# Layer 2 ffn of a four-layer graph network: layernorm folded into the product, sum with the tanh on GpSimd

## Chip, cores and metric

One core of a Trainium2 chip runs the whole network. The metric is device time in microseconds of one execution. The engines are TensorE (PE; its weight loads are listed as PEld), VectorE (DVE), ScalarE (ACT), GpSimd (POOL) and SyncE (SP, which starts most transfers).

## What is computed

Four layers, each a graph part and a feed-forward part, act on X, 2,708 tokens of 256 features in f32; every part is fed with the layernorm of X and its result is added to X. The change touches only layer 2's feed-forward part, which applies one step thirty times to each token by itself:

```python
def step(h, _):
    h = h + 0.01 * jnp.tanh(h)
    h = h * jax.nn.sigmoid(h)
    h = _layernorm(h, ln_w, ln_b)
    h = jnp.einsum('bsc,dc->bsd', h, W) + b
    return (h, None)
x, _ = jax.lax.scan(step, x, None, length=N_ITERS)   # N_ITERS = 30
```

`_layernorm` subtracts the row's mean, multiplies by 1 / sqrt(variance + 1e-5), then by ln_w, and adds ln_b.

## The kernel before

X lies in SBUF as 22 tiles of 128 tokens by 256 features (tokens on partitions, `NT = 22`). The parts run one after the other in the code (`PHASES`), but the instructions of neighbouring parts overlap. The kernel is written in a tile framework: it records operations in program order with their dependencies, and a scheduler then fixes the order of each engine's queue before the run. This order need not be that of the code. On the chip every engine takes its own queue strictly in that order, and a waiting instruction holds up those behind it.

`l2_ffn` keeps the state in `Hs`, 22 tiles, and treats them as 11 pairs (`G = 11`); thirty steps make `ITERS * G = 330` pairs. First ln_w is multiplied into the weight (`Ww`), and ln_b times the weight is added to the bias. `layernorm` then fills Hs. Each pair runs through `s_tanh` and six stages, which hand their result on in `st`:

- `s_tanh` (L558): tanh of the pair on ACT, 128x512, into a buffer `th`.
- `s_silu` (L562, L563): DVE computes 0.01 th + hs in one instruction, ACT takes silu of it in place.
- `s_stats` (L570 to L572, and L114 through the helper `pow`): for each tile DVE's statistics and their aggregate give mean and variance (`sc_mv`); POOL adds epsilon and raises to the power -0.5 (`sc_r`).
- `s_norm` (L579, L581, L582): DVE computes -mean * r (`sc_m`); ACT normalizes the first tile of the pair, POOL the second, into `n`.
- `s_turn` (L590, L593): four transposes on PE into PSUM (`psT`), one copy on ACT to SBUF (`nT`).
- `s_mix` (L600): four products of 128x128 by 128x256 on PE, listed as eight MATMUL, into one PSUM tile (`psN`).
- `s_bias` (L117 through the helper `tt`): DVE adds the bias on reading PSUM and writes hs.

The loop goes over ticks. In tick T the stages are called for pairs T-6, T-4, T-5, T-3, T-2, T-1 in this order, then s_tanh for pair T:

```python
for tick in range(total + len(stages)):
    for k in (6, 4, 5, 3, 2, 1):
        if 0 <= tick - k < total:
            st[tick - k] = stages[k - 1](tick - k, st[tick - k])
    if tick < total:
        st[tick] = s_tanh(tick)
```

After the loop, 11 additions on DVE (L117) put Hs onto X. All `th`, `n` and `nT` come from one pool of 11 buffers (`two`); psT and psN have four PSUM buffers each; the small `sc_` tiles have four. A pair of tiles reads what was written for it 11 ticks earlier.

Of the kernel before, what the change touches and what calls it, by code (L numbers as in the profile page):

```python
# [37 lines left out]
class Net:  # L38
    """Tokens lie on partitions: token n is row n % 128 of tile n // 128. X is the residual stream."""
# [40 lines left out]
    def bcast(self, name, n, tag=None, pool=None, row=0):  # L80
        """A row of an input on every partition."""
        src = self.a[name]
        pool = pool or self.const
        t = pool.tile([P, n], F32, name="bc_" + name, tag=tag or "bc_" + name)
        self.nc.sync.dma_start(
            t, bass.AP(tensor=src.tensor, offset=src.offset + row * n, ap=[[0, P], [1, n]])
        )
        return t

    def cols(self, name, k):  # L90
        """An input that the host laid out as [128, k]."""
        t = self.const.tile([P, k], F32, name="co_" + name, tag="co_" + name)
        self.nc.sync.dma_start(t, self.a[name])
        return t

    def mat(self, src, k, n, tag, pool=None):
        """A [k * 128, n] matrix with its rows on partitions."""
        t = (pool or self.wp).tile([P, k, n], F32, name=tag, tag=tag, bufs=3 if tag in ("w1", "w2") else 2)
        self.nc.sync.dma_start(t, src.rearrange("(k p) n -> p k n", p=P))
        return t  # L100

    def pair(self, name, shape=(2, D), parts=P):
        """Room for two tiles of tokens."""
        t = self.two.tile([P, 2 * D], F32, name=name, tag="two")
        t = t[:parts, : int(np.prod(shape))]
        return t if len(shape) == 1 else t.rearrange("p (a b) -> p a b", b=shape[1])

# [17 lines left out]
    def moments(self, mv, g0, g1):  # L125
        """Mean and variance of each token of tiles g0..g1 of X."""
        nc = self.nc
        for t in range(g0, g1):
            p = rows(t)
            st = self.tmp.tile([P, 6], F32, name="bst", tag="bst", bufs=4)  # L130
            nc.vector.bn_stats(st[:p], self.X[:p, t, :])
            nc.vector.bn_aggr(mv[:p, t, :], st[:p])

    def layernorm(self, scale_of, sink=None, into=None):
        """For each pair of tiles: sink(t0, scaled (x - mean), as [128, 2, 256]); kept in `into`."""
# [18 lines left out]
    def rstd(self, out, var, g0, g1):  # L154
        """1 / sqrt(var + eps)."""
        ve = self.tmp.tile([P, g1 - g0], F32, name="ve", tag="ve")
        self.ts(ve, var, EPS, ALU.add)
        self.pow(out, ve, self.mhalf)

    def transpose_into(self, ZT, gamma=None, beta=None):  # L160
        """A sink that puts the features of a pair of tiles on partitions."""
# [22 lines left out]
    def token_matmul(self, ZT, W, t, n, m=P):  # L184
        """Tile t's rows times W [128, 2, n], on token partitions."""
        ps = self.psB.tile([P, n], F32, name="psM", tag="psB")
        for c in range(KD):
            self.nc.tensor.matmul(ps[:m], lhsT=ZT[:, c, t * P : t * P + m], rhs=W[:, c, :],  # L188
                                  start=(c == 0), stop=(c == KD - 1))
        return ps  # L190

# [1 line left out]
    def chunk_dma(self, b, j0, move):  # L193
        """Calls move(m, c) for each part of a chunk: m cuts it from an [N, N] matrix, c from a tile."""
# [9 lines left out]
    def adj_chunks(self, b, src):  # L204
        """Chunks of src [N, N] for output tokens of block b: (first row tile, tile, parts)."""
# [8 lines left out]
    def aggregate(self, weights, R, w, done, src=None):  # L214
        """sum_j weights[j, i] R[j]; weights(b, j0, adj tile, parts, n) gives the chunk's weights."""
# [25 lines left out]
    def ramp(self, E):  # L241
        """E, E - 1, ... 1 on every partition: the earlier expert is the larger."""
        r = self.const.tile([P, E], F32, name=f"rev{E}", tag=f"rev{E}")
        self.nc.gpsimd.iota(r, pattern=[[-1, E]], base=E, channel_multiplier=0,
                            allow_small_or_imprecise_dtypes=True)
        return r
# [7 lines left out]
    def first_max(self, l, E, rev, m, oh, at=None):  # L254
        """The largest of E and a one-hot of its first place."""
# [9 lines left out]
    def top2(self, l, E):  # L265
        """Weights of all experts: softmax over the two largest, 0 elsewhere."""
# [31 lines left out]
    def logits(self, lhs, rhs, bias, E):  # L298
        """lhs: per tile, the chunks of stationary operands; rhs: the chunks of moving ones."""
# [11 lines left out]
    def add_weighted_bias(self, wf, name, E):  # L311
        """X += sum_e w_e b_e."""
# [19 lines left out]
    def hidden(self, W, src, kc, nh, n, func, bias, tag, k0=0):  # L332
        """func(W.T src + bias), features on partitions: nh blocks of 128 by n tokens."""
# [11 lines left out]
    def add_expert(self, h, nh, W, b0, k, wf, e):  # L345
        """X += w_e (h.T W) for the k tiles from b0."""
# [11 lines left out]
    def l0_gnn(self):  # L358
# [29 lines left out]
        def reciprocals(b, j0, at, parts, n):  # L388
            """1 / r of layer 1's weights, with r >= 1 as 0 and 1e-18 added to every r: it changes
            only those whose weight, exp(-2 (1/r - 1)^2), is 0 anyway."""  # L390
# [141 lines left out]
    def l2_ffn(self):  # L532
        nc, a = self.nc, self.a
        ITERS = 30
        lw, lb = self.cols("L2_ffn_ln_w", KD), self.cols("L2_ffn_ln_b", KD)
        bias = self.bcast("L2_ffn_b", D, tag="rowbc")
        WT = self.mat(a["L2_ffn_WT"], KD, D, "w3")
        # (n w + lb) W.T + b = n (w W.T) + (lb W.T + b), n the normalized row.
# [6 lines left out]
        Ww = self.const.tile([P, KD, D], F32, name="Ww", tag="Ww")  # L545
        for c in range(KD):
            self.ts(Ww[:, c, :], WT[:, c, :], lw[:, c : c + 1], ALU.mult)

        Hs = self.big.tile([P, NT, D], F32, name="Hs", tag="R")
        self.layernorm(self.rstd, into=Hs)  # L550
        G = NT // 2
        st = {}
        hs = lambda s: Hs[:, 2 * (s % G) : 2 * (s % G) + 2, :]
        tiny = lambda name, shape: self.tmp.tile([P, *shape], F32, name=name, tag=name, bufs=4)

        def s_tanh(s):
            th = self.pair("th")
            nc.scalar.activation(th, hs(s), AF.Tanh)  # L558
            return th

        def s_silu(s, th):
            nc.vector.scalar_tensor_tensor(th, th, 0.01, hs(s), op0=ALU.mult, op1=ALU.add)  # L562
            nc.scalar.activation(th, th, AF.Silu)  # L563
            return th

        def s_stats(s, g):
# [5 lines left out]
            nc.gpsimd.tensor_scalar(r, mv[:, :, 1], EPS, 1.0, op0=ALU.add, op1=ALU.mult)  # L572
            self.pow(r, r, self.mhalf)
            return g, mv, r

        def s_norm(s, gmr):
            g, mv, r = gmr
            m = tiny("sc_m", (2,))
            nc.vector.scalar_tensor_tensor(m, mv[:, :, 0], -1.0, r, op0=ALU.mult, op1=ALU.mult)  # L579
            n = self.pair("n")  # L580
            nc.scalar.activation(n[:, 0, :], g[:, 0, :], AF.Identity, bias=m[:, 0:1], scale=r[:, 0:1])  # L581
            nc.gpsimd.tensor_scalar(n[:, 1, :], g[:, 1, :], r[:, 1:2], m[:, 1:2], op0=ALU.mult,  # L582
                                    op1=ALU.add)
            return n

        def s_turn(s, n):
            ps = self.psB.tile([P, KD, 2 * P], F32, name="psT", tag="psB")
            for c in range(KD):
                for j in range(2):
                    nc.tensor.transpose(ps[:, c, j * P : (j + 1) * P], n[:, j, c * P : (c + 1) * P],  # L590
                                        self.ident)
            nT = self.pair("nT", (KD, 2 * P))
            nc.scalar.copy(nT, ps)  # L593
            return nT

        def s_mix(s, nT):
            ps = self.psA.tile([P, 2, D], F32, name="psN", tag="psA")
            for j in range(2):
                for c in range(KD):
                    nc.tensor.matmul(ps[:, j, :], lhsT=nT[:, c, j * P : (j + 1) * P],  # L600
                                     rhs=Ww[:, c, :], start=(c == 0), stop=(c == KD - 1))
            return ps

        def s_bias(s, ps):
            self.tt(hs(s), ps, bias.unsqueeze(1).to_broadcast([P, 2, D]), ALU.add)

        stages = [s_silu, s_stats, s_norm, s_turn, s_mix, s_bias]
        total = ITERS * G
        for tick in range(total + len(stages)):
            # A pair's transposes go before the products of the pair ahead, which cover their copy.  # L610
            for k in (6, 4, 5, 3, 2, 1):
# [4 lines left out]
        for t0 in range(0, NT, 2):  # L616
            self.tt(self.X[:, t0 : t0 + 2, :], Hs[:, t0 : t0 + 2, :], self.X[:, t0 : t0 + 2, :],
                    ALU.add)

# [1 line left out]
    def artanh(self, out, x):  # L621
        """0.5 (log1p(x) - log1p(-x)), log1p(u) = ln(w) u / (w - 1) with w = 1 + u (u where w is 1)."""
# [18 lines left out]
    def tanh_over(self, out, n, raw):  # L641
        """out = tanh(n) / n with n = max(raw, 1e-15)."""
# [6 lines left out]
    def ball(self, f, raw):  # L649
        """The factor that brings a row of norm raw into the ball: min(1, maxnorm / norm)."""  # L650
# [4 lines left out]
    def log_factor(self, out, f, raw):  # L655
        """artanh(n) / n, n = max(f * raw, 1e-15): the factor of logmap0 for a row of norm f * raw."""
# [14 lines left out]
    def l3_gnn(self):  # L671
# [6 lines left out]
        # The bias as a point of the ball.  # L678
# [12 lines left out]
        # mx = z W.T, its squared norm and its product with the bias.  # L691
# [12 lines left out]
        # |z| = sqrt(D var) / sqrt(var + eps)  # L704
# [17 lines left out]
        # Moebius sum of s mx and hb: ca mx + cb hb.  # L722
# [38 lines left out]
        # expmap0, proj, logmap0, relu, expmap0, proj: one factor of relu(u) for each token.  # L761
# [19 lines left out]
    def l3_ffn(self, out):  # L781
# [30 lines left out]
        # Each token's place among its expert's tokens, counted from 1.  # L812
# [20 lines left out]
        # A token past the capacity is written to a row of its own that no expert reads.  # L833
# [124 lines left out]
```

## Time and profile before

| quantity | us |
|---|---|
| three runs | 3749.0, 3742.19, 3748.62 |
| their median | 3748.62 |
| span of the profiled execution, first to last instruction | 3735.1 |
| difference of the median to the span | 13.5 |
| first tanh of the loop / last start of a product (L600) | 2075.1 / 2975.3 |

The profiled execution's time outside its span is not listed by the profile; the three runs lie 7.1 to 13.9 us above the span.

In the window 2100 to 2900 us, in the middle of the loop, the engines are busy, out of 800 us: PE 743.9, DVE 659.3, ACT 665.9, POOL 574.3, at a granted TensorE clock of 1.00. The mean durations there, in us, of one instruction:

| line, engine | what | number | one |
|---|---|---|---|
| L600 PE | product, 128x256 | 2640 | 0.380 |
| L590 PE | transpose, 128x128 | 1320 | 0.294 |
| L570 DVE | statistics, 128x256 | 660 | 0.405 |
| L571 DVE | aggregate | 660 | 0.169 |
| L562 DVE | 0.01 th + hs, 128x512 | 330 | 0.686 |
| L117 DVE | bias, 128x512 from PSUM | 330 | 0.671 |
| L579 DVE | sc_m, 128x2 | 330 | 0.161 |
| L558, L563 ACT | tanh, silu, 128x512 | 330 each | 0.615, 0.624 |
| L581 ACT | n, 128x256 | 330 | 0.600 |
| L593 ACT | copy, 128x512 from PSUM | 330 | 0.586 |
| L582 POOL | n, 128x256 | 330 | 0.801 |
| L572 POOL | epsilon, 128x2 | 330 | 0.413 |
| L114 POOL | power, 128x2 | 330 | 0.699 |

Durations of neighbours on one engine overlap somewhat: the next instruction starts before the last has left the engine. In the lists of waits a line reads: engine, tile and line that waited, the releaser, total us, times, longest us. In a timeline or a chain: start us, duration us, engine, tile, line. In the page's slices each digit is the busy share of one fortieth of the span, in tenths.

### The profile page before, as it was taken

The page shows a single profiled execution, that of the slowest core. Times are in us where ns is not written, and L with a number is a line of the kernel's source. Part 1 is how long each engine was busy: PE and PEld are TensorE (multiplying, and loading weights), DVE is VectorE, ACT ScalarE, POOL GpSimd, SP SyncE. Part 2 cuts the span into 40 slices and gives each one's busy share as a digit, 9 for nine tenths or more (in the row PEclk, how much of TensorE's full clock was granted, in tenths as well). Part 3 has the DMA queues.
Part 4 walks back from the last instruction along what each step waited for, and adds up shares of the span by engine and source line. Part 5 has one row for each costly group of instructions (what it writes and reads, how often), then busy time and mean ns, then how long its engine had stood idle before and what let it go on. Part 6 is the DMA issues. An engine that isn't in the chain of part 4 may idle for free.

```text
span 3735.1 us, 38081 instructions
## 1 busy us (share of the span) xinstructions
PE 3315.3 (89%) x13384; PEld 2346.6 (63%) x13384; DVE 1721.5 (46%) x4185; ACT 1445.2 (39%) x2458; POOL 931.8 (25%) x1224
## 2 busy tenths in 40 slices
PE   7988989999999999999999899999999859945782
PEld 5655556666667885555688566666666648733551
DVE  6999982111113112211401688888888850040005
ACT  2433451121222463222200588888888630011110
POOL 3323220000000000000200477777777510021004
PEclk9999987999999998999999999999999979957896
DMA  4333330000000352000154100000000015402222
GB/s 150 128 116 123 125 99 31 12 23 12 12 6 12 113 147 60 9 15 17 41 145 128 32 1 1 1 1 1 1 1 1 2 31 143 119 10 76 88 78 68
DMA packets 135083, 203.52 MB, mean 54 GB/s; under 512 B 10699, under 2 KB 59685, under 8 KB 134893
## 3 DMA queue, kind: packets, MB, share of 16 engines
q1 hardware_dynamic: 132812, 195.54, 17.4%
q0 software_dynamic: 2080, 5.55, 0.4%
q8 instruction: 106, 1.74, 0.2%
q14 instruction: 85, 0.69, 0.1%
HBM read 159.23 MB, written 41.83 MB: 54 GB/s over the span
## 4 chain that ended last, share of the span: by engine, by line
PE 55%; POOL 17%; DVE 14%; issue 9%; DMA 4%; ACT 1%; POOLq 0%; SPq 0%; DVEq 0%; ACTq 0%
PE acc L223 20%; PE psH L340 17%; PE psY L352 11%; POOL sc_r L114 6%; POOL n L582 5%; DVE sc_bs L570 4%; POOL sc_r L572 4%; DMA xb<-slots 3%; DVE inv L396 3%; PE psY L877 2%; DVE sc_m L579 1%; POOL e L413 1%; PE psS L406 1%; PE psY L325 1%; PE psM L188 1%
## 5 line engine op out<-in xcount | busy, mean ns | idle before, releaser
L223 PE MATMUL acc<-R,adj 128*128 128x256 f32 (+3 forms) x2904 | 654.3, 383 | 35.9 <-DVE R L121 35.9
L223 PEld LDWEIGHTS acc<-R,adj 128*128 128x128 f32 (+3 forms) x2904 | 527.0, 186 | 162.9 <-issue 51.3
L600 PE MATMUL psN<-Ww,nT 128*128 128x256 f32 x2640 | 625.9, 380 | 0.7 <-ACT nT L593 0.7
L600 PEld LDWEIGHTS psN<-Ww,nT 128*128 128x128 f32 x2640 | 476.8, 191 | 52.4 <-ACT nT L593 1.1
L354 DVE SCALAR_TENSOR_TENSOR X<-psY,wf,X 128x256 f32<-128x256 f32 x308 | 147.3, 483 | 756.2 <-PE psY L352 756.2
L342 ACT ACTIVATE hA<-psH,co_L_ffn_b 128x512 f32<-128x512 f32 (+2 forms) x256 | 164.3, 642 | 761.0 <-PE psH L340 761.0
L340 PE MATMUL psH<-ZT,w 128*128 128x512 f32 (+1 forms) x1056 | 435.9, 562 | 0.0
L114 POOL TENSOR_TENSOR lnscale<-ve,mhalf 128x4 f32<-128x4 f32 (+1 forms) x36 | 34.8, 965 | 1509.2 <-DVE ve L121 1502.3
L396 DVE RECIPROCAL inv<-inv 128x1024 f32<-128x1024 f32 (+3 forms) x72 | 377.8, 5285 | 5.7 <-ACT inv L395 5.4
L590 PE MATMUL psT<-ident,n 128*128 128x128 f32 x1320 | 254.1, 294 | 76.4 <-POOL n L582 39.0
L340 PEld LDWEIGHTS psH<-ZT,w 128*128 128x128 f32 x1056 | 201.9, 192 | 184.7 <-issue 176.3
L352 PE MATMUL psY<-w,hA 128*128 128x256 f32 x1408 | 311.7, 379 | 0.0
L352 PEld LDWEIGHTS psY<-w,hA 128*128 128x128 f32 x1408 | 267.5, 190 | 53.4 <-issue 19.1
L582 POOL TENSOR_SCALAR n<-th,sc_r,sc_m 128x256 f32<-128x256 f32 x330 | 264.3, 801 | 133.3 <-DVE sc_m L579 66.0
L590 PEld LDWEIGHTS psT<-ident,n 128*128 128x128 f32 x1320 | 143.9, 140 | 238.2 <-ACT n L581 165.5
L558 ACT ACTIVATE th<-Hs 128x512 f32<-128x512 f32 x330 | 202.9, 615 | 220.6 <-DVE Hs L123 220.6
L223 PE MATMUL acc<-R,e 128*128 128x257 f32 x968 | 238.3, 398 | 51.5 <-POOL e L413 29.9
L223 PEld LDWEIGHTS acc<-R,e 128*128 128x128 f32 x968 | 180.2, 192 | 119.5 <-POOL e L413 59.1
L570 DVE BATCH_NORM_STATS2 sc_bs<-th 128x6 f32<-128x256 f32 x660 | 252.9, 405 | 0.0
L562 DVE SCALAR_TENSOR_TENSOR th<-th,Hs 128x512 f32<-128x512 f32 x330 | 226.3, 686 | 24.7 <-ACT th L558 24.7
L114 POOL TENSOR_TENSOR sc_r<-sc_r,mhalf 128x2 f32<-128x2 f32 x330 | 230.7, 699 | 27.5
L581 ACT ACTIVATE n<-th,sc_m,sc_r 128x256 f32<-128x256 f32 x330 | 198.0, 600 | 85.4 <-DVE sc_m L579 75.0
(259 smaller groups left out, 3750.3 us busy)
## 6 DMA issues: line engine op xcount, KB each, us to landing
adj<-in_adjT SPq DMA_DIRECT2D x150, 512.0 KB
inv<-inv SPq DMA_DIRECT2D x50, 512.0 KB
adj<-inv SPq DMA_DIRECT2D x50, 512.0 KB
w<-in_L_ffn_w SPq DMA_DIRECT2D x32, 512.0 KB
w<-in_L_ffn_W SPq DMA_DIRECT2D x16, 512.0 KB
w<-in_L_ffn_expert_w SPq DMA_DIRECT2D x18, 256.0 KB
adj<-in_adjT SPq DMA_DIRECT2D x30, 148.0 KB
adj<-in_adjT SPq DMA_DIRECT2D x15, 256.0 KB
```

The lines of the kernel that those rows point to most:

```text
L114: self.nc.gpsimd.tensor_tensor(out, base, half[:, :k], op=ALU.pow)
L223: nc.tensor.matmul(acc[s][:ps, :w], lhsT=wt[:pj, k, s * P : s * P + ps], rhs=R[:pj, jt, :w], start=(jt == 0), stop=(jt == NT - 1))
L340: nc.tensor.matmul(ps, lhsT=W[:, c, f * P : (f + 1) * P], rhs=src(c), start=(c == 0), stop=(c == kc - 1))
L352: nc.tensor.matmul(py, lhsT=h[:, f, j * P : (j + 1) * P], rhs=W[:, f, :], start=(f == 0), stop=(f == nh - 1))
L396: nc.vector.reciprocal(o, o)
L558: nc.scalar.activation(th, hs(s), AF.Tanh)
L562: nc.vector.scalar_tensor_tensor(th, th, 0.01, hs(s), op0=ALU.mult, op1=ALU.add)
L570: nc.vector.bn_stats(bs, g[:, j, :])
L581: nc.scalar.activation(n[:, 0, :], g[:, 0, :], AF.Identity, bias=m[:, 0:1], scale=r[:, 0:1])
L582: nc.gpsimd.tensor_scalar(n[:, 1, :], g[:, 1, :], r[:, 1:2], m[:, 1:2], op0=ALU.mult, op1=ALU.add)
L590: nc.tensor.transpose(ps[:, c, j * P : (j + 1) * P], n[:, j, c * P : (c + 1) * P], self.ident)
L600: nc.tensor.matmul(ps[:, j, :], lhsT=nT[:, c, j * P : (j + 1) * P], rhs=Ww[:, c, :], start=(c == 0), stop=(c == KD - 1))
```

## The change

The mean is no longer subtracted from the rows: since the product is linear, the columns of the scaled weight are centred once ahead of the loop (`V`, by a product with a constant 1/256 and a subtraction), so that a row's mean drops out of the product. The factor r of each row is applied when PSUM is read, together with the bias: `s_out` is one DVE instruction per tile, psN * r + bias. `s_norm` is gone, and the transposes read the output of silu. The statistics go into `s_turn`; epsilon is added on ACT, the power stays on POOL.

The state Hs is kept 100 times as large (`UP`): then the sum is th + hs without a factor, and GpSimd computes it in a stage of its own (`s_sum`); tanh and silu scale their input by 1/100 in the same instruction, and V and the bias carry the factor 100. The scale of the first layernorm carries it too. The stages are now s_sum, s_silu, s_turn, s_mix, s_out, called for T-5, T-3, T-4, T-2, T-1. The addition to X is done by DVE in s_out of the last step, with 1/100.

```diff
         self.tt(bias, ps, bias, ALU.add)
-        Ww = self.const.tile([P, KD, D], F32, name="Ww", tag="Ww")
+        self.ts(bias, bias, UP, ALU.mult)
+        V = self.const.tile([P, KD, D], F32, name="V", tag="V")
         for c in range(KD):
-            self.ts(Ww[:, c, :], WT[:, c, :], lw[:, c : c + 1], ALU.mult)
+            self.ts(V[:, c, :], WT[:, c, :], lw[:, c : c + 1], ALU.mult)
+        mean = self.pair("mean", (P,))
+        self.ts(mean, self.ones, 1.0 / D, ALU.mult)
+        ps = self.psB.tile([P, D], F32, name="psM", tag="psB")
+        for c in range(KD):
+            nc.tensor.matmul(ps, lhsT=mean, rhs=V[:, c, :], start=(c == 0), stop=(c == KD - 1))
+        for c in range(KD):
+            self.tt(V[:, c, :], V[:, c, :], ps, ALU.subtract)
+            self.ts(V[:, c, :], V[:, c, :], UP, ALU.mult)
+
+        eps = self.const.tile([P, 1], F32, name="eps", tag="eps")
+        nc.gpsimd.memset(eps, EPS)
...
-        self.layernorm(self.rstd, into=Hs)
+        def scale(out, var, g0, g1):
+            self.rstd(out, var, g0, g1)
+            self.ts(out, out, UP, ALU.mult)
+
+        self.layernorm(scale, into=Hs)
...
-            nc.scalar.activation(th, hs(s), AF.Tanh)
+            nc.scalar.activation(th, hs(s), AF.Tanh, scale=1.0 / UP)
             return th
 
+        def s_sum(s, th):
+            nc.gpsimd.tensor_tensor(th, th, hs(s), op=ALU.add)
+            return th
+
         def s_silu(s, th):
-            nc.vector.scalar_tensor_tensor(th, th, 0.01, hs(s), op0=ALU.mult, op1=ALU.add)
-            nc.scalar.activation(th, th, AF.Silu)
+            nc.scalar.activation(th, th, AF.Silu, scale=1.0 / UP)
             return th
 
-        def s_stats(s, g):
+        def s_turn(s, g):
             mv, r = tiny("sc_mv", (2, 2)), tiny("sc_r", (2,))
...
-            nc.gpsimd.tensor_scalar(r, mv[:, :, 1], EPS, 1.0, op0=ALU.add, op1=ALU.mult)
+            nc.scalar.activation(r, mv[:, :, 1], AF.Identity, bias=eps)
             self.pow(r, r, self.mhalf)
-            return g, mv, r
-
-        def s_norm(s, gmr):
-            g, mv, r = gmr
-            m = tiny("sc_m", (2,))
-            nc.vector.scalar_tensor_tensor(m, mv[:, :, 0], -1.0, r, op0=ALU.mult, op1=ALU.mult)
-            n = self.pair("n")
-            nc.scalar.activation(n[:, 0, :], g[:, 0, :], AF.Identity, bias=m[:, 0:1], scale=r[:, 0:1])
-            nc.gpsimd.tensor_scalar(n[:, 1, :], g[:, 1, :], r[:, 1:2], m[:, 1:2], op0=ALU.mult,
-                                    op1=ALU.add)
-            return n
...
-                    nc.tensor.transpose(ps[:, c, j * P : (j + 1) * P], n[:, j, c * P : (c + 1) * P],
+                    nc.tensor.transpose(ps[:, c, j * P : (j + 1) * P], g[:, j, c * P : (c + 1) * P],
                                         self.ident)
...
-        def s_bias(s, ps):
-            self.tt(hs(s), ps, bias.unsqueeze(1).to_broadcast([P, 2, D]), ALU.add)
-
-        stages = [s_silu, s_stats, s_norm, s_turn, s_mix, s_bias]
+        def s_out(s, pr):
+            ps, r = pr
+            for j in range(2):
+                nc.vector.scalar_tensor_tensor(hs(s)[:, j, :], ps[:, j, :], r[:, j : j + 1], bias,
+                                               op0=ALU.mult, op1=ALU.add)
+            if s >= (ITERS - 1) * G2:
+                x = self.X[:, 2 * (s % G2) : 2 * (s % G2) + 2, :]
+                nc.vector.scalar_tensor_tensor(x, hs(s), 1.0 / UP, x, op0=ALU.mult, op1=ALU.add)
+
+        stages = [s_sum, s_silu, s_turn, s_mix, s_out]
...
-            for k in (6, 4, 5, 3, 2, 1):
+            for k in (5, 3, 4, 2, 1):
...
-        for t0 in range(0, NT, 2):
-            self.tt(self.X[:, t0 : t0 + 2, :], Hs[:, t0 : t0 + 2, :], self.X[:, t0 : t0 + 2, :],
-                    ALU.add)
```

`G2` is the former `G`, `gT` the former `nT`. What else the diff holds are comments.

More of the change, by code (lines that the diff above doesn't have):

```diff
@@ L534, in l2_ffn @@
         ITERS = 30
+        UP = 100.0
         lw, lb = self.cols("L2_ffn_ln_w", KD), self.cols("L2_ffn_ln_b", KD)
@@ L544, in l2_ffn @@
         self.tt(bias, ps, bias, ALU.add)
-        Ww = self.const.tile([P, KD, D], F32, name="Ww", tag="Ww")
+        self.ts(bias, bias, UP, ALU.mult)
+        V = self.const.tile([P, KD, D], F32, name="V", tag="V")
         for c in range(KD):
-            self.ts(Ww[:, c, :], WT[:, c, :], lw[:, c : c + 1], ALU.mult)
-        Hs = self.big.tile([P, NT, D], F32, name="Hs", tag="R")
-        self.layernorm(self.rstd, into=Hs)
-        G = NT // 2
+            self.ts(V[:, c, :], WT[:, c, :], lw[:, c : c + 1], ALU.mult)
[9 more added lines that the diff above has]
+        nc.gpsimd.memset(eps, EPS)
+        Hs = self.big.tile([P, NT, D], F32, name="Hs", tag="R")
+        def scale(out, var, g0, g1):
+            self.rstd(out, var, g0, g1)
+            self.ts(out, out, UP, ALU.mult)
+        self.layernorm(scale, into=Hs)
+        G2 = NT // 2
         st = {}
-        hs = lambda s: Hs[:, 2 * (s % G) : 2 * (s % G) + 2, :]
+        hs = lambda s: Hs[:, 2 * (s % G2) : 2 * (s % G2) + 2, :]
         tiny = lambda name, shape: self.tmp.tile([P, *shape], F32, name=name, tag=name, bufs=4)
@@ L571, in s_stats @@
                 nc.vector.bn_aggr(mv[:, j, :], bs)
-            nc.gpsimd.tensor_scalar(r, mv[:, :, 1], EPS, 1.0, op0=ALU.add, op1=ALU.mult)
+            nc.scalar.activation(r, mv[:, :, 1], AF.Identity, bias=eps)
             self.pow(r, r, self.mhalf)
-            return g, mv, r
-        def s_norm(s, gmr):
-            g, mv, r = gmr
-            m = tiny("sc_m", (2,))
-            nc.vector.scalar_tensor_tensor(m, mv[:, :, 0], -1.0, r, op0=ALU.mult, op1=ALU.mult)
-            n = self.pair("n")
-            nc.scalar.activation(n[:, 0, :], g[:, 0, :], AF.Identity, bias=m[:, 0:1], scale=r[:, 0:1])
-            nc.gpsimd.tensor_scalar(n[:, 1, :], g[:, 1, :], r[:, 1:2], m[:, 1:2], op0=ALU.mult,
-                                    op1=ALU.add)
-            return n
-        def s_turn(s, n):
             ps = self.psB.tile([P, KD, 2 * P], F32, name="psT", tag="psB")
@@ L589, in s_turn, with s_mix @@
                 for j in range(2):
-                    nc.tensor.transpose(ps[:, c, j * P : (j + 1) * P], n[:, j, c * P : (c + 1) * P],
+                    nc.tensor.transpose(ps[:, c, j * P : (j + 1) * P], g[:, j, c * P : (c + 1) * P],
                                         self.ident)
[L592 to L596, printed above, removed]
+            gT = self.pair("gT", (KD, 2 * P))
+            nc.scalar.copy(gT, ps)
+            return gT, r
+        def s_mix(s, gr):
+            gT, r = gr
             ps = self.psA.tile([P, 2, D], F32, name="psN", tag="psA")
@@ L599, in s_mix @@
                 for c in range(KD):
-                    nc.tensor.matmul(ps[:, j, :], lhsT=nT[:, c, j * P : (j + 1) * P],
-                                     rhs=Ww[:, c, :], start=(c == 0), stop=(c == KD - 1))
-            return ps
-        def s_bias(s, ps):
-            self.tt(hs(s), ps, bias.unsqueeze(1).to_broadcast([P, 2, D]), ALU.add)
-        stages = [s_silu, s_stats, s_norm, s_turn, s_mix, s_bias]
-        total = ITERS * G
+                    nc.tensor.matmul(ps[:, j, :], lhsT=gT[:, c, j * P : (j + 1) * P],
+                                     rhs=V[:, c, :], start=(c == 0), stop=(c == KD - 1))
+            return ps, r
+        def s_out(s, pr):
[7 more added lines that the diff above has]
+        stages = [s_sum, s_silu, s_turn, s_mix, s_out]
+        total = ITERS * G2
         for tick in range(total + len(stages)):
-            for k in (6, 4, 5, 3, 2, 1):
+            for k in (5, 3, 4, 2, 1):
                 if 0 <= tick - k < total:
```

## The prediction

> **What bounds the kernel now.** First the page's busy shares in 40 slices, to place the change in time.
>
> ```profile
> PE   7988989999999999999999899999999859945782
> ...
> DVE  6999982111113112211401688888888850040005
> ACT  2433451121222463222200588888888630011110
> POOL 3323220000000000000200477777777510021004
> PEclk9999987999999998999999999999999979957896
> ```
>
> Slices 24 to 31 are the only long stretch in which four engines are all busy: with parts of their neighbours this is the loop of layer 2's ffn (first tanh at 2075.1 us, last product at 2975.9), 330 pairs of tiles. PE shows 9, but that share is modelled, so I read who waits, in the window 2100:2900.
>
> ```profile
> PEld psT L590 <- ACT n L581: 137.2, 297, 1.0
> DVE sc_m L579 <- POOL sc_r L114: 117.4, 299, 0.5
> POOL sc_r L572 <- DVE sc_mv L571: 67.8, 150, 0.8
> ACT n L581 <- DVE sc_m L579: 66.9, 149, 0.5
> PEld psT L590 <- POOL n L582: 66.2, 158, 0.4
> ```
>
> PE waits for the normalized rows n, those for sc_m, and that for the power on POOL. Then the chain of waits for a few microseconds out of the middle:
>
> ```profile
> 2440.28 0.20 POOL sc_r L572
> ...
> 2440.56 0.72 POOL sc_r L114
> ...
> 2441.30 0.17 DVE sc_m L579
> ...
> 2441.66 1.06 POOL n L582
> ...
> 2442.80 0.65 POOL sc_r L572
> ...
> 2443.53 0.71 POOL sc_r L114
> ...
> 2444.26 0.16 DVE sc_m L579
> 2444.42 0.66 DVE sc_bs L570 x2
> ...
> 2445.64 0.20 POOL sc_r L572
> ```
>
> No PE is in it: statistics, epsilon, power, sc_m and n hand over between DVE and POOL, and the picture repeats after 2445.64 - 2440.28 = 5.36 us, two pairs: **2.68 us a pair**, and 330 x 2.683 = 885 us. How fast PE could go is seen at the loop's start, while pairs are still in store: its transposes begin at 2094.68, 2096.85 and 2099.01, so **2.16 us a pair**. The clock there is 1.00 in the window's row.
>
> **The change, part by part.** Durations are from the group rows unless said.
>
> *Removed, per pair.* On POOL L572 (0.41) and L582 (0.80); on DVE L562 (0.69), L579 (0.16) and the wide L117 (0.67); on ACT L581 (0.60). With them goes the loop shown above: the power's result is now read only by s_out, two stages later, and the transposes read g itself. What is late next is worked out below.
>
> *Added, per pair.* (1) POOL: th + hs, 128x512 with two SBUF inputs. The nearest rows are the same shape: L526 1.27 (median, DVE running beside it) and L413 1.27. I take 1.27. (2) ACT: epsilon onto 128x2. Not in the trace; ACT's 128x22 takes 0.22, its 128x256 0.42 to 0.60. I take 0.20; at 0.42 the round trip below grows by 0.22, 0.11 a pair. (3) DVE: two s_out from PSUM, 128x256; L383 has exactly this form, 0.48 each, and successive ones may start about 0.40 apart (the wide ones, 0.68 long, let the next start after 0.61). The scales 1/100 on Tanh and Silu ride in the same instruction: nothing.
>
> *Sums per pair after.* PE unchanged, 2.16. POOL 1.27 + 0.70 + two gaps of 0.08 (as between L582 and L572) = 2.13. ACT 0.62 + 0.62 + 0.59 + 0.20 = 2.03. DVE 2 x 0.31 + 2 x 0.09 + 2 x 0.48 = 1.76 (statistics by their starting distances). Nobody needs more than 2.16, against 2.68 now: the sums allow 0.52 x 330 = 172 us. PE and POOL are within 0.03 of each other, so waits decide what is left of it.
>
> *The added waits.* In POOL's queue the power of a pair stands ahead of a later pair's sum; it waits for r on ACT. Who waits behind it: the sum, then silu, then all. As the code orders it, power(s) goes in the tick in which sum(s+2) goes, so the round trip covers two pairs: sum 1.27, hand-over 0.05 (2120.44 to 2120.49, ACT to PE), silu 0.62, 0.05, two statistics and aggregates 0.87 (0.31 + 0.09 + 0.31 + 0.16 by the starts 2123.37, 2123.68 and 2123.76), 0.08, r 0.20, POOL's waking 0.20 (sc_m ended 2441.46, n began 2441.66), power 0.70, 0.09: **4.13 us, or 2.07 a pair** with nothing in the way. In its way on ACT can be a copy (0.48 from start to next start), as silu follows a copy in every second pair now: 4.61, **2.31 a pair**. I take that. The trace of before can't show the order in each queue after: it isn't the code's order even now (the wide L117, first in a tick by the code, runs behind the aggregates, at 2123.76 after 2123.68). So the bounds are 2.16 below and, above, the round trips in the rivals.
>
> *The port.* POOL's n takes 0.56 us at 2122.91 beside statistics, 1.06 at 2119.95 beside L562; its 128x2 L572 takes 0.19 and 0.64 likewise. So the removed L562, with two SBUF inputs, held POOL up by 0.45 to 0.50. The wide L117, with one input in PSUM, ran at 2121.60 beside a power of 0.70, the power's usual length. s_out is of that second kind, so I charge no contention. That POOL can hold DVE up too shows at 1821.60: four L123, SBUF to SBUF, take 2.33 us beside L526, 1.38 without it (2980.36). The Trainium skill, SBUF — State Buffer, section Who interferes with whom, has that rule: a VectorE instruction with two SBUF inputs locks a GpSimd one that reads SBUF out, one with at most one such input doesn't. It says nothing of the scalar column r, which s_out reads as well; if that counted, the last rival below would hold.
>
> *Against the change* stands first the row: the sum costs POOL 1.27 where DVE spent 0.69. The skill's GPSIMD Engine Reference, section Engine selection, tells one not to put two-input elementwise work on GpSimd at all; by its figure for 2,048 elements (section Elementwise — side-by-side cycle accounting: 4497 ns, a quarter is an estimated 1.12) POOL's sum of terms would be 1.98 instead of 2.13, and by its advice the move would be undone. Here POOL's total, not the single duration, is what counts.
>
> *Start and end.* Added ahead of the loop on DVE: bias 0.35, mean 0.80 (L542's shape), two subtractions 0.43, two scalings 0.35 = 2.7 us, and six of 0.16 on the scales, 3.7 in all; on PE four half-products, 0.9. DVE idles 23 us before 2073.45 and covers what doesn't need PE; uncovered it costs 3.7, and some four early sums beside the 18 instructions of L123 (5.90 us from 2075.38) could hold these up by 1 us each. Against that, the first L562 waits behind those 18 now, and the first transposes come at 2088.39, 13.3 us after the first tanh; the sum on POOL isn't behind them, and the power, sc_m and n (2086.48 to 2088.41) drop out ahead of PE: up to 9 us gained. I take 0 (bounds -9 and +8). At the end the 11 additions to X (0.68) lie between other DVE work now, and do so after: 0.
>
> **The sum.** 330 x (2.31 - 2.683) = -123 us. The profiled execution's span is 3735.1, so 3612 after; the three runs lie 7.1 to 13.9 us above that span, and their median of 3748.62 13.5. With the same 13.5 outside the span: **3626 us**, 3.3% less.
>
> **Rivals.**
>
> *A. PE sets the pace.* The order lets enough pairs stand in store, and each takes 2.16 as at 2094.68 to 2099.01: -173, **3576 us**. For it: the sums, and eleven buffers of pairs. Against: in the middle of the loop only 3 or 4 pairs lie between tanh and copy (by time 2601 195 tanh, 191 copies), and POOL's 2.13 leaves no slack.
>
> *B. The same round trip, with s_out in its way on DVE.* One of the two (0.40) ahead of the statistics: 5.01, 2.51 a pair, -57, **3692 us**. Both: 5.41, 2.70, which is about no change.
>
> *C. Slower: the round trip through PE takes the place.* If DVE takes s_out of an older pair ahead of each pair's statistics, as the code has it, and ACT takes r and copy ahead of silu, then: hand-over 0.05, transposes and products 2.38 (2123.46 to 2125.84), 0.05, two s_out 0.80, statistics 0.87, 0.08, r 0.20, copy 0.48, silu 0.62 = 5.53 for two pairs, **2.77 a pair**: +27, **3776 us**. It decides from 5.37 us for two pairs on. For it: both orders are the code's, and r is a new wait in ACT's queue with copy, silu and tanh behind it. Against: the queues are not in the code's order now.
>
> *D. Slower by the port.* If s_out counts as two SBUF readers, it and the sum exclude one another: POOL 2.13 + 0.80 = 2.93, +82, **3831 us**. Against: the undisturbed L117.
>
> *E. The change doesn't reach the end:* something else holds 2.68 (B with both). Within 0.2%, 7.5 us, which is about what a measurement can tell from no change here: 3748.
>
> **Chances.** Forecast (2.22 to 2.42 a pair) 0.40; A 0.17; B 0.14; E 0.04; C 0.16; D 0.09. Faster: 0.40 + 0.17 + 0.14 = 0.71; same 0.04; slower 0.25. The range takes in A below (3576) and C above (3776), with some of the start's bounds 3570 to 3785; D and what lies past either end, some 0.15 to 0.2, is left out.
>
> **What would show it.** Right: POOL's 128x512 sum at 1.27 and its power at 0.70, POOL the busiest or level with PE, the transposes waiting for silu, and that for POOL's sum; the start of successive transposes 2.3 apart. A: PE without idle before L590's successor, POOL with gaps. B: statistics starting right behind s_out. C: in the chain PE, s_out, statistics, r, silu in turn, with ACT idle before r. D: sums of over 1.7 us, or s_out over 0.7. My number is wrong above all if the order in a queue puts a waiting instruction ahead of one that PE needs.

## The result, and the profile after

The changed kernel takes **3845.39 us** (median of four runs), the kernel before 3745.40 beside it: ratio 1.0268, interval 1.025 to 1.0286. That is 100 us slower; 3626 was forecast, with a range of 3570 to 3785.

The first lines are the page's slices of the changed kernel, to be held against those of before.

```profile
PE   7988889999999999999999788888888849955782
...
DVE  6999972111113012112303555555555660040005
ACT  2433441212122652222101666666666640110110
POOL 3222320000000000000102666666666620012004
```

VectorE falls from 8 to 5 and ScalarE from 8 to 6: the work that the change removes is gone, and the loop is longer. No engine is full, PE included, so something is waited for. The list of waits in the window 2100:2900 (engine, tile and line that waited, releaser, total us, times, longest us):

```profile
DVE sc_bs L592 <- ACT th L585: 326.5, 258, 1.3
POOL th L581 <- ACT th L577: 280.3, 262, 1.1
ACT th L585 <- POOL th L581: 277.2, 264, 1.5
PEld psN L610 <- ACT gT L602: 219.5, 265, 1.6
PE psN L610 <- ACT gT L602: 156.4, 265, 1.4
```

The second and the third line stand against each other: GpSimd's sum (L581) waits for tanh (L577), and silu (L585) on the same ScalarE waits for the sum, each in nearly every pair (262 and 264 times among the window's 265 sums). The chain of waits in the middle of the loop shows the whole circle; "issue" is a stretch for which the view names no work:

```profile
2501.52 1.28 POOL th L581
2502.80 0.02 issue
2502.82 0.02 ACT th L585
2502.85 0.51 issue
2503.36 0.57 ACT gT L602
2503.93 0.54 ACT th L577
2504.47 0.07 issue
2504.53 1.28 POOL th L581
```

From sum to sum it is 2504.53 - 2501.52 = **3.01 us, and that is one pair**. ScalarE's own queue says why. In its timeline the columns are start, duration, engine, line, operation, and in brackets the idle time before:

```profile
2502.82 0.63 ACT L585 ACTIVATE th<-th 128x512 f32<-128x512 f32 x1 [1.05 <-POOL th L581]
2503.36 0.57 ACT L602 COPY gT<-psT 128x512 f32<-128x512 f32 x1
2503.82 0.63 ACT L577 ACTIVATE th<-Hs 128x512 f32<-128x512 f32 x1
2504.49 0.29 ACT L594 ACTIVATE sc_r<-sc_mv,eps 128x2 f32<-128x2 f32 x1
2505.84 0.63 ACT L585 ACTIVATE th<-th 128x512 f32<-128x512 f32 x1 [1.05 <-POOL th L581]
```

The tanh at 2503.82 is that of the very pair whose silu comes next, at 2505.84: the sum starts 0.07 us after that tanh ends, and silu 0.02 after the sum. So ScalarE does silu of pair s (0.54 until the next start), an older pair's copy (0.46), tanh of pair s+1 (0.63), hands over (0.07), waits out the sum (1.28 and 0.02) and only then has silu of s+1: 3.00. The 1.05 us of idling before each silu is what r (L594) leaves of the sum. Nothing is in store between tanh, sum and silu. From GpSimd's own timeline it is seen what the power does meanwhile:

```profile
2504.53 1.27 POOL L581 TENSOR_TENSOR th<-th,Hs 128x512 f32<-128x512 f32 x1 [1.08 <-ACT th L577]
2505.76 0.71 POOL L114 TENSOR_TENSOR sc_r<-sc_r,mhalf 128x2 f32<-128x2 f32 x1
2507.55 1.27 POOL L581 TENSOR_TENSOR th<-th,Hs 128x512 f32<-128x512 f32 x1 [1.08 <-ACT th L577]
```

The power at 2505.76 belongs to the pair whose sum began at 2501.52: counted from the start of the loop, it stands behind the next pair's sum and ahead of that of the pair after. It is done at 2506.47, and GpSimd then idles for 1.08 us, until that pair's tanh is done.

The loop takes 330 pairs x (3.013 - 2.683) = 109 us more (3.013 us is the distance of successive sums in the window). The start gives some of it back: from VectorE's last additions of the stage ahead to the loop's first product it is 6.2 us (2084.29 to 2090.5), before the change 16.7 (2073.45 to 2090.2). That makes about 98 of the 100 us measured. The spans of the two profiled executions differ by more, 111.6, because the stage ahead, whose instructions are the same, ends 10.8 us later in this trace; in the runs below it ends 2 to 11 us later than in the trace of before, and why isn't shown.

### The profile page after: what moved, and what is told of

Read it like the earlier page. It is cut to its first block, busy times and chain, and to the rows that moved or that the text cites. A ratio compares the mean times of both kernels' runs of the same rounds, so it can differ in the third digit from the quotient of the medians.

```text
span 3846.7 us, 37759 instructions
## 1 busy us (share of the span) xinstructions
PE 3308.4 (86%) x13388; PEld 2384.0 (62%) x13388; DVE 1577.3 (41%) x3867; ACT 1343.7 (35%) x2458; POOL 941.6 (24%) x895
## 4 chain that ended last, share of the span: by engine, by line
PE 54%; POOL 13%; issue 12%; ACT 11%; DVE 7%; DMA 4%; SPq 0%; POOLq 0%; DVEq 0%; ACTq 0%
PE acc L223 20%; PE psH L340 17%; PE psY L352 11%; POOL th L581 11%; ACT gT L602 5%; ACT th L577 4%; DMA xb<-slots 3%; DVE inv L396 3%; PE psY L890 2%; PE psS L406 1%; PE psY L325 1%; POOL e L413 1%; PE psM L188 1%; DVE inv L394 1%; PE psL L305 1%
## 5 line engine op out<-in xcount | busy, mean ns | idle before, releaser
L610 PE MATMUL psN<-V,gT 128*128 128x256 f32 x2640 | 659.8, 393 | 192.5 <-ACT gT L602 192.5
L610 PEld LDWEIGHTS psN<-V,gT 128*128 128x128 f32 x2640 | 475.8, 190 | 321.7 <-ACT gT L602 270.2
L581 POOL TENSOR_TENSOR th<-th,Hs 128x512 f32<-128x512 f32 x330 | 419.5, 1271 | 372.8 <-ACT th L577 371.4
L585 ACT ACTIVATE th<-th 128x512 f32<-128x512 f32 x330 | 207.7, 630 | 341.8 <-POOL th L581 341.6
L577 ACT ACTIVATE th<-Hs 128x512 f32<-128x512 f32 x330 | 208.3, 631 | 221.8 <-DVE Hs L123 221.7
L617 DVE SCALAR_TENSOR_TENSOR Hs<-psN,sc_r,bc_L_ffn_b 128x256 f32<-128x256 f32 x660 | 283.3, 471 | 5.7 <-POOL sc_r L114 4.9
L406 PE MATMUL psS<-ZT 128*128 128x512 f32 (+2 forms) x528 | 213.6, 550 | 0.0
L413 POOL TENSOR_TENSOR e<-e,adj 128x1024 f32<-128x1024 f32 (+3 forms) x72 | 139.3, 1939 | 295.1 <-ACT e L412 277.9
```

Source lines behind the costliest of these rows:

```text
L406: nc.tensor.matmul(ps[:p, :n], lhsT=ZT[:, c, j : j + p], rhs=ZT[:, c, b * TB : b * TB + n], start=(c == 0), stop=(c == KD - 1))
L577: nc.scalar.activation(th, hs(s), AF.Tanh, scale=1.0 / UP)
L581: nc.gpsimd.tensor_tensor(th, th, hs(s), op=ALU.add)
L585: nc.scalar.activation(th, th, AF.Silu, scale=1.0 / UP)
L610: nc.tensor.matmul(ps[:, j, :], lhsT=gT[:, c, j * P : (j + 1) * P], rhs=V[:, c, :], start=(c == 0), stop=(c == KD - 1))
L617: nc.vector.scalar_tensor_tensor(hs(s)[:, j, :], ps[:, j, :], r[:, j : j + 1], bias, op0=ALU.mult, op1=ALU.add)
```

## Experiments

Theory L: this loop over one pair, through ScalarE's queue and the sum, sets the pace. Theory P, the forecast's rival C: the round trip through TensorE and s_out. Theory G: GpSimd has too much work altogether. All are edits of the changed kernel unless said.

### The sum on half a pair

```diff
-            nc.gpsimd.tensor_tensor(th, th, hs(s), op=ALU.add)
+            nc.gpsimd.tensor_tensor(th[:, 0, :], th[:, 0, :], hs(s)[:, 0, :], op=ALU.add)
```

> The changed kernel, with GpSimd adding only the first tile of each pair (the second tile's th is passed on without the sum, so that part of the computation is left out). Theory L (a loop over one pair: silu, copy, tanh on ScalarE, sum on GpSimd, silu of the next pair; 3.01 us a pair): the sum falls from 1.27 to about 0.75 us and the pair from 3.01 to 2.49, 330 x 0.52 = 172 us off, about 3675. Theory P (the round trip through TensorE and s_out, my rival C): the sum isn't in it, 3.01 stays, about 3845. Theory G (GpSimd is just too slow in total, 1.27 + 0.71): as L or less, since GpSimd is left with 1.5 of work, about 3675.

Measured: 3667.29 us, 178 less than the changed kernel. Its chain, as above:

```profile
2401.85 0.74 POOL th L581
2402.59 0.02 issue
2402.61 0.63 ACT th L585
2403.24 0.47 ACT gT L602
2403.72 0.54 ACT th L577
2404.25 0.07 issue
2404.32 0.74 POOL th L581
```

The same circle in 2.47 us (the view gives silu its 0.63 here and called most of it "issue" above); the sum's 0.54 saved is found in each pair in full. P is out; L and G stay.

### The copy on VectorE

```diff
-            nc.scalar.copy(gT, ps)
+            nc.vector.tensor_copy(gT, ps)
```

> The changed kernel, with the copy of the transposes from PSUM on VectorE in place of ScalarE. Theory L: the copy's 0.46 us leaves the loop, 3.01 to about 2.55, 330 x 0.46 = 152 us off, about 3693. Theory P: the copy stays in the round trip through TensorE, on another engine; unchanged within 30 us, about 3845. Theory G: GpSimd has the same work, about 3845.

Measured: 3694.05 us. GpSimd's work is the same and 151 us are gone, which G can't give. The amount is that of L, but it proves less than it seems to: in the middle of the loop PE (566 us busy of 600) stands in the chain at every second tanh, so a second limit was close at 2.53 us.

### A buffer of its own for silu

tanh and sum get five buffers of the tag `ea`, which layer 0 used; silu writes to a buffer of the pool `two` instead of in place.

```diff
-            th = self.pair("th")
+            th = self.tmp.tile([P, 2, TB], F32, name="th", tag="ea", bufs=5)
+            th = th[:, 0, :].rearrange("p (a b) -> p a b", b=D)
...
-            nc.scalar.activation(th, th, AF.Silu, scale=1.0 / UP)
-            return th
+            g = self.pair("g")
+            nc.scalar.activation(g, th, AF.Silu, scale=1.0 / UP)
+            return g
```

> The changed kernel, with tanh and sum in buffers of their own (five, from a tag that layer 0 used) and silu writing to a second buffer, nothing else. The queue on ScalarE then holds the tanh of a pair two or three pairs ahead of its silu (it is next to it in the changed kernel). Theory L: no loop over one pair is left, the pace is that of TensorE or GpSimd, 2.2 to 2.35 us a pair, 3580 to 3630. Theory P and theory G: the same work on the same engines in the same stages, about 3845.

Measured: 3614.43 us, 3.4% less than before (0.966, 0.9644 to 0.9676). No instruction is added or taken away; only the buffers, and by them the order that the scheduler fixes. The chain is PE alone:

```profile
2401.93 0.44 PE psT L601 x4
2402.37 1.73 PE psN L612 x8
2404.10 0.44 PE psT L601 x4
2404.53 1.73 PE psN L612 x8
```

2.17 us a pair, the pace read off the start of the old loop. In ScalarE's queue a tanh now stands four pairs ahead of its silu: behind the loop's last tanh, at 2793.88, five silus still follow, the fifth its own. P and G fall; L holds. But 330 x (3.013 - 2.165) = 280 us were to be expected, and 231 came. From first to last product the loop gained 269 (994.5 to 725.2); the rest was lost after it. Behind the loop the trace shows SyncE's queue busy with transfers of a zero tile, and the bias of the next stage behind them:

```profile
2797.07 59.84 SPq L809 DMA_DIRECT2D slots<-zero  x8
2857.01 8.99 SPq L85 DMA_DIRECT2D bc_L_gnn_bias<-in_L_gnn_bias  x1
```

ScalarE then waits 40.88 us for that bias. In the kernel before, the zeros are issued from 542.9 to 596.6, and the bias meets a free queue:

```profile
2976.68 0.34 SPq L85 DMA_DIRECT2D bc_L_gnn_bias<-in_L_gnn_bias  x1
```

Layer 3's zero tile has the tag `ea` as well. In this run GpSimd fills it only at 2796.10, right behind the loop's last sum.

### The same with another tag

```diff
-            th = self.tmp.tile([P, 2, TB], F32, name="th", tag="ea", bufs=5)
+            th = self.hp.tile([P, 2, TB], F32, name="th", tag="hB", padded_shape=[P, 2, TB], bufs=3)
```

> As the experiment with silu's own buffer, but tanh and sum use three buffers of the tag of layer 1's hidden rows, which nothing needs later, in place of the five that layer 3's zero tile waits for. The queue on ScalarE holds a pair's tanh two pairs ahead of its silu. Theory L: pace of TensorE, 2.165 us a pair as before, and the 38 us in which the stage after the loop waited for the bias behind the late zero transfers go: 3614 - 38 = 3576. If the 38 us have another cause, 3614 stays; if three buffers are too few, more than 2.3 us a pair and over 3620.

Measured: **3574.85 us**, 0.9545 of before (0.9529 to 0.9561): 39.6 us less than with `ea`. This is the fastest version, faster than both kernels. The bias is issued in 0.34 us again (at 2815.17), so the zero transfers were the cause. In ScalarE's queue a tanh now stands two pairs ahead of its silu (three silus follow the last tanh, at 2802.83). GpSimd is busy for 541.8 of 600 us, and hardly anything waits for it:

```profile
2399.37 0.71 POOL L114 TENSOR_TENSOR sc_r<-sc_r,mhalf 128x2 f32<-128x2 f32 x1 [0.21 <-ACT sc_r L596]
2400.04 1.29 POOL L582 TENSOR_TENSOR th<-th,Hs 128x512 f32<-128x512 f32 x1
```

### The halves of the change alone

First the sum back on VectorE, as an addition of its own:

```diff
-            nc.gpsimd.tensor_tensor(th, th, hs(s), op=ALU.add)
+            nc.vector.tensor_tensor(th, th, hs(s), op=ALU.add)
```

> The changed kernel, with the sum th + hs on VectorE in place of GpSimd (undoes one half of the change). Theory L: the sum takes 0.69 in place of 1.27, and the queue on ScalarE has the tanh one to two pairs ahead; 2.2 to 2.4 us a pair, 3580 to 3645. Theory G: also faster, by all that GpSimd cost: 2.2 to 2.4. Theory P: slower than the changed kernel or equal, since VectorE has 0.6 more in the round trip, 3845 or more.

Measured: 3650.27 us, 5 us over the upper end: 2.39 us a pair from the first to the last product, with VectorE busy for 559 us of 600.

Then the fold alone, with 0.01 th + hs in one instruction on VectorE as before:

```diff
-        UP = 100.0
+        UP = 1.0
...
-            nc.scalar.activation(th, th, AF.Silu, scale=1.0 / UP)
+            nc.vector.scalar_tensor_tensor(th, th, 0.01, hs(s), op0=ALU.mult, op1=ALU.add)
+            nc.scalar.activation(th, th, AF.Silu)
...
-        stages = [s_sum, s_silu, s_turn, s_mix, s_out]
+        stages = [s_silu, s_turn, s_mix, s_out]
...
-            for k in (5, 3, 4, 2, 1):
+            for k in (4, 2, 3, 1):
```

> The changed kernel without the move of the sum: 0.01 th + hs in one instruction on VectorE as before, state not scaled up, layernorm folded. Theory L: GpSimd has only the power, no loop over one pair through it; about the pace of the sum on VectorE (3650), 3600 to 3660. Theory P (fold itself costs, through s_out or through r in ScalarE's queue): slower than before, over 3750.

Measured: 3646.93 us, 0.9743 of before (0.9727 to 0.976). The fold gains 95 us by itself; the move of the sum turns that into a loss of 100.

Then the sum alone, as an edit of the kernel before: the state scaled by 100 as in the change, and

```diff
-            nc.vector.scalar_tensor_tensor(th, th, 0.01, hs(s), op0=ALU.mult, op1=ALU.add)
-            nc.scalar.activation(th, th, AF.Silu)
+            nc.scalar.activation(th, th, AF.Silu, scale=1.0 / UP)
...
+        def s_sum(s, th):
+            nc.gpsimd.tensor_tensor(th, th, hs(s), op=ALU.add)
+            return th
```

> The kernel before with the state scaled by 100 and the sum on GpSimd, layernorm not folded. GpSimd then has 1.27 + 0.41 + 0.71 + 0.80 = 3.2 us a pair and becomes the bound by its sum alone: at least 3.2 + 4 gaps of 0.08 = 3.5 against 2.68, 330 x 0.8 = 270 us more, 4010 or over. If GpSimd's load didn't matter but only the order, less than 3.0 us a pair, under 3850.

Measured: 4048.81 us (1196 us from the first to the last product, 3.62 a pair). The amount is as expected, but not for the reason expected: GpSimd is busy for only 443.2 of 600 us, 2.7 a pair. Its epsilon takes 0.19 and its n 0.56 here, not 0.41 and 0.80, and in every two pairs it waits 1.29 and 0.44 us for the statistics:

```profile
2403.86 1.26 POOL L568 TENSOR_TENSOR th<-th,Hs 128x512 f32<-128x512 f32 x1
2405.12 0.56 POOL L591 TENSOR_SCALAR n<-th,sc_r,sc_m 128x256 f32<-128x256 f32 x1
2406.97 0.19 POOL L581 TENSOR_SCALAR sc_r<-sc_mv 128x2 f32<-128x2 f32 x1 [1.29 <-DVE sc_mv L580]
```

The chain there goes back and forth over two pairs, 7.26 us: two sums, n and power on GpSimd, silu, copies and n on ScalarE, the transposes on TensorE. So here too the sum costs by being waited for, in another circle, and that the sum of GpSimd's work came near the time is luck.

Last the fold alone with buffers as in the fastest version:

```diff
+            th = self.hp.tile([P, 2, TB], F32, name="th", tag="hB", padded_shape=[P, 2, TB], bufs=3)
+            th = th[:, 0, :].rearrange("p (a b) -> p a b", b=D)
...
+            nc.vector.scalar_tensor_tensor(th, th, 0.01, hs(s), op0=ALU.mult, op1=ALU.add)
+            g = self.pair("g")
+            nc.scalar.activation(g, th, AF.Silu)
+            return g
```

> The fold alone (sum in one instruction on VectorE), with silu writing to a buffer of its own and tanh in three buffers, as in the fastest run so far. If GpSimd's part of the sum is worth something beside TensorE's pace: VectorE then needs 0.61 more a pair, 2.4, and this run is slower than 3575 by 20 us or more. If TensorE's 2.165 a pair is the end in either case: 3575 within 10 us, and the move of the sum brings nothing.

Measured: 3641.07 us. VectorE is busy for 576 us of 600 in the middle of the loop; that its load sets the pace (2.36 us a pair from the first to the last product) is likely but not shown, since the chain there is PE almost throughout. So with the loop opened the sum on GpSimd is worth 3641 - 3575 = 66 us; the same move costs 3845 - 3647 = 198 us with the buffers of the change.

### tanh earlier in the code

```diff
+        LEAD = 2
+        for s in range(LEAD):
+            st[s] = s_tanh(s)
         for tick in range(total + len(stages)):
+            if tick + LEAD < total:
+                st[tick + LEAD] = s_tanh(tick + LEAD)
             for k in (5, 3, 4, 2, 1):
...
-            if tick < total:
-                st[tick] = s_tanh(tick)
```

> The changed kernel with tanh called first in each tick and for the pair two ticks ahead; buffers as they were. In ScalarE's queue tanh still stands right ahead of the silu of the same pair, after silu and copy of older pairs. Theory L (the queue's order decides): unchanged, 3.01 us a pair, 3830 to 3855. If the code's distance between tanh and silu decided, as my prediction's round trip over two pairs has it: 2.2 to 2.4 a pair, 3580 to 3650.

Measured: 3834.03 us, the same circle of 3.01 us in the chain. Two pairs of distance in the code are not two pairs in the queue.

### The copy in buffers of its own

```diff
-            gT = self.pair("gT", (KD, 2 * P))
+            gT = self.hp.tile([P, 2, TB], F32, name="gT", tag="hB", padded_shape=[P, 2, TB], bufs=3)
+            gT = gT[:, 0, :].rearrange("p (a b) -> p a b", b=2 * P)
```

> The changed kernel with the copy of the transposes in three buffers of its own; th as it was, silu in place. ScalarE's queue becomes silu, r (of an older pair), tanh of the next pair, copy, silu of that pair. Theory L: r takes the copy's place in the loop, and the copy runs beside the sum: silu 0.53, r 0.19, tanh 0.54, hand-over 0.07, sum 1.28, 0.02 = 2.63 us a pair in place of 3.01, 330 x 0.38 = 125 us off, about 3720. If the buffers as such, and not the order, made the difference in the run with silu's own buffer: 3575 to 3615.

Measured: 3801.73 us, a miss by 80. That buffers alone don't do it is clear, but the pace is 2.93 us and not 2.63. GpSimd's and ScalarE's timelines:

```profile
2400.68 1.26 POOL L581 TENSOR_TENSOR th<-th,Hs 128x512 f32<-128x512 f32 x1
2402.93 0.70 POOL L114 TENSOR_TENSOR sc_r<-sc_r,mhalf 128x2 f32<-128x2 f32 x1 [0.99 <-PE psN L611]
2403.61 1.26 POOL L581 TENSOR_TENSOR th<-th,Hs 128x512 f32<-128x512 f32 x1
```

```profile
2401.98 0.63 ACT L585 ACTIVATE th<-th 128x512 f32<-128x512 f32 x1 [1.13 <-POOL th L581]
2402.51 0.28 ACT L594 ACTIVATE sc_r<-sc_mv,eps 128x2 f32<-128x2 f32 x1
2402.70 0.61 ACT L577 ACTIVATE th<-Hs 128x512 f32<-128x512 f32 x1
```

The tanh ends at 2403.31, yet the sum starts at 2403.61, right behind the power. The power began 0.14 us after r ended (2402.79), r follows silu on ScalarE, and silu the sum. The circle is sum 1.28, 0.02, silu 0.53, r 0.28, 0.14, power 0.68 = 2.93, which I had left out. The list names PE as the power's releaser. That is probably chance: two waits stand ahead of the power in GpSimd's queue, for r and for the next sum, and the second starts 0.10 us after the first here, as it does in the changed kernel, where PE held nothing up. This circle goes through the power like the forecast's, but not through the statistics: the r that follows silu is that of an older pair, so it closes with every pair, where the forecast's trip covers two.

### Epsilon on GpSimd again

```diff
-            nc.scalar.activation(r, mv[:, :, 1], AF.Identity, bias=eps)
+            nc.gpsimd.tensor_scalar(r, mv[:, :, 1], EPS, 1.0, op0=ALU.add, op1=ALU.mult)
```

> The changed kernel with epsilon added on GpSimd again, so that r leaves ScalarE's queue. Theory L: r isn't in the loop (it stands behind tanh, which the sum waits for), unchanged, 3.01 us a pair, 3835 to 3850. If the new wait in ScalarE's queue for r costs (my rival C): 0.3 us less a pair, about 3745.

Measured: 3844.32 us. In the changed kernel r isn't on the way: it runs beside the sum.

## Why the prediction was wrong

- **What failed is the step on who waits for whom, in the part on the added waits: "Who waits behind it: the sum, then silu, then all."** The forecast let only the power hold the sum up, and put the sum's wait for tanh at nothing. That wait decides: tanh stands on ScalarE behind the silu and the copy of earlier pairs, and that silu waits for the sum before. The circle has neither the power nor the statistics in it and takes 3.01 us a pair, where 2.31 was forecast.
- The trip that the forecast did price is there, and over two pairs as it said: from the sum at 2501.52 to the end of that pair's power at 2506.47 it is 4.95 us, against 4.61 forecast. But the next sum behind that power starts only at 2507.55, so the trip is hidden.
- Why the wait was missed: in the code, tanh of pair s+2 is called right after silu of pair s, so this circle would cover two pairs, 1.5 us each, and be hidden. In the queue it is tanh of pair s+1. The forecast saw that the queues weren't in the code's order, said so, and left this open. It also read that "3 or 4 pairs lie between tanh and copy"; three lie there after the change too (172 tanh begun, 169 copies by time 2601), but none of them between tanh and silu. With two pairs there (the same with another tag) the pace is 2.165. That ScalarE's tanh and silu of a pair have GpSimd between them was in the diff; before, VectorE had the middle one, at 0.69.
- Rival C forecast slower, but by other work: with half the sum, which isn't in C, the time fell by 178 us. Rival D's 3831 lies near the 3845 measured by luck: its cause, the port, isn't there, since beside s_out the sum took 1.27 (1.265 to 1.345), s_out 0.47. Rival A was the right pace for the work: 3576 against the 3575 measured with the buffers opened.
- Most terms were right: sum 1.27 (1.27 forecast), power 0.71 (0.70), s_out 0.47 (0.48), PE's pace 2.165 (2.16). r was low, 0.295 against 0.20. The start was taken at 0 and gained 10.6 us, a little past the forecast's bound of 9. The 13.5 us "outside the span" are hardly that: a run of the changed kernel took 3848.49 with a span of 3846.7, so most of the 13.5 is the difference of one execution to another.
- On the port, the forecast gives the Trainium skill's rule (SBUF — State Buffer, section Who interferes with whom) without its exception: the page frees a VectorE instruction with one SBUF input only outside the 2-port modes. The forecast's own row of L123, which has one such tensor and was held up (2.33 against 1.38 us), doesn't fit the rule as it was given.
- Against the advice of the Trainium skill, GPSIMD Engine Reference, section Engine selection, the move to GpSimd does pay here, 66 us, once it isn't waited for. In the changed kernel as it stands the advice would have been right by 198 us, and there the sum's length does count, because it stands in the circle: with 0.73 us in place of 1.27, 178 us were gone.

What stays open: why the scheduler puts tanh so late. That the buffers decide it is shown (no other edit in two runs); the rule by which they do isn't. In both runs tanh stood as many pairs ahead as there were buffers for it, less one (five buffers, four pairs; three buffers, two pairs). Both changed two things at once, buffers of their own for tanh and one for silu's result; which of them opens the loop isn't separated.

## What to carry to other kernels

When work of one engine is moved to a second and comes back to the first, look for the circle: what stands in the first engine's queue between the return of one item and the sending of the next. Its length is divided by the number of items between sending and return in the queue, and that number must be read from the queue, not from the code; while the engines' sums leave room, the longest such circle decides. Buffers can tie the two ends together: here buffers of their own for tanh and for silu's result freed them. A borrowed buffer must be checked for who needs it next.

## What the hardware showed that was not expected

- ScalarE needs 0.295 us for 128x2 elements in the changed kernel, about half of what it needs for 128x512 (0.63).
- Eight transfers of zeros kept SyncE's queue for 59.84 us, and a small load behind them took a further 14.6 us to land (chain of the first run with silu's own buffer, from 2857.01).
- GpSimd's power begins 0.08 us after r ends on ScalarE in the fastest run (r at 2401.18 for 0.28, power at 2401.54), and 0.14 us after it in the run with the copy's own buffers, where a second wait stands between. The sum begins 0.07 us after tanh, while silu begins on ScalarE 0.02 us after GpSimd's sum.
